# One planned order for all five engines of a four-layer attention kernel, in place of the scheduler's order and a few pins

## The chip, the cores and the metric

One core of a Trainium2 chip. The metric is the device time of one launch in microseconds (us); the kernel before takes 2680.95 us, the median of three runs (2679.22 to 2687.39).

## The reference

An input of 16 samples, each of 256 channels and 32 x 32 positions in float32, goes through four layers, one sample independent of the next. Cut to what matters:

```python
# L0: group norm (8 groups), attention over 1024 positions, projection, residual
xn = group_norm(x, gamma, beta)
q, k, v = split(w_qkv @ xn + b_qkv)
x = w_proj @ (softmax(q.T @ k / 16) applied to v) + b_proj + x
# L1: a gate per position, from the mean and the maximum over the channels
w3 = relu(conv3x3([mean_c(x), max_c(x)], w1, b1))
x = x * sigmoid(conv3x3(mean_c(x) + max_c(x) + w3, w2, b2))
# L2: the same as L0 with its own norm and weights
x = x + wp @ attention(wq @ h, wk @ h, wv @ h) + bp,   h = group_norm(x)
# L3: attention with 32-wide q and k, logits clipped, no norm
energy = clip((Wq @ x + bq).T @ (Wk @ x + bk) * 32**-0.5, -10, 10)
x = gamma[0] * (softmax(energy) applied to Wv @ x + bv) + x
```

## The kernel before

**Weights.** The weights are folded once at the start: the query and key weights of L0 and L2 into one matrix `m`, the value and projection weights into `wvp` (`fold`, `fold3`). A matrix for the 3x3 convolutions, `toep`, is built on POOL from an index table `tidx` (L91 to L101).

**Products.** Nearly all matrix products are made by the Strassen-Winograd scheme: seven products of half-size blocks in place of eight, with sums of blocks before and after. `product` (L577) issues the matmuls; `seven` issues the products of a group in turn, with the names of their PSUM banks: b, a, c, f, with a letter ahead for the stage (sb, sa, sc, sf for the logits, tb, ta, tc, tf for the first projection, vb and so on for the values; b, af, c for the weighted sum). A finished bank is copied to SBUF by ACT (L696 in the logits) or added to a block by DVE (L627 in the logits; L749 in the weighted sum). There are eight banks of PSUM, taken in turn.

**One sample.** `head` loads x (L0's channels, and again as tokens `xr`) and normalises it. `sample` then runs L0's `attend`, the gate of L1, `send`, the group norm of L2, L2's `attend`, `send` again, and L3. In `attend`, `combine` (L924 to L927, DVE) makes the sums `xs` of x's blocks; tb, tc and the others make `t`; `values` makes `vt`; then for each half of the positions `logits` (copies L696, sums L627, exponentials L706 and L708 on ACT) is followed by `weighted` (sums L722, L723, L768, L774 of the exponentials on DVE, copies on ACT, sums L749, and `done`, L754, which scales and adds to the residual). Each half h ends with `then(h, ...)`. In the gate, mean and maximum come from ACT (L1043) and DVE (L1035), and the product with the gate is L1061 on DVE and L1065 on ACT.

**From tokens to channels.** L2 needs channels where L1 left tokens. `turn` transposes with DVE (L525), and `send` writes a half of the sample to DRAM in four pieces and fetches it back in the other layout, all from SP's queue:

```python
            for g in range(NG):
                nc.sync.dma_start(          # L536: mid_x <- t_z or t_l, 128 KB
            ...
            nc.sync.dma_start(              # L540: x <- mid_x, 512 KB
```

**Group norm.** `group_norm` is a chain, most of it on DVE: four `bn_stats` (L114, one for each half and channel block), two aggregates (L117), small steps L119 to L134 with two transposes, then one power on POOL (L138), then three small steps (L141, L143, L144), and the normalisation itself, one half of the channels on DVE (L147) and one on ACT (L150). TensorE's tb product reads what L147 wrote.

**The order of the work.** Even and odd samples are two streams, generators that yield after each product; `in_turn` takes one step of each by turns, the odd stream 30 steps behind (`OFFSET`). Constants `W_...` put further steps between stages. Small tasks without a fixed place, the bias adds (L493, ACT) and the DVE transposes of tokens (L500), are `chores` that are taken one for each step. So the program is written down ("traced") in one order, and from there a scheduler sets each engine's order by its own estimates. It is bound in a few places only: `keep_in_program_order` holds the instructions it is given in their traced order (the building of `toep` on POOL, sample 1's `bn_stats`, the copies of `whole`, parts of `fold3`, a square for the checks on sizes); `behind_folds` puts sample 0's L150 behind the copies of the folded weights on ACT; and `in_traced_order` ties TensorE, DVE and ACT to the traced order in the last sample's `ending`, where the order was written out by hand (L1188 are sums there).

Of the kernel before, what the change touches and what calls it, by code (L numbers as in the profile page):

```python
# [13 lines left out]
ALU = mybir.AluOpType  # L14
AX = mybir.AxisListType

P = 128
C = 256
CC = C // P
# [4 lines left out]
TPH = HALF // P  # L24
GROUP = 32
DQK = 32
G4 = P // DQK
PH = P // 2
# [11 lines left out]
L2_GAMMA, L2_BETA, L2_BQ, L2_BK, L2_BP = range(5, 10)  # L40
NVEC = 10
OFFSET = 30


W_PLANES, W_GATE1, W_GATE2, W_SEND1, W_NORM1, W_NORM2, W_NORM3, W_SEND2, W_EXP, W_AV, W_AV3 = 9, 1, 2, 4, 2, 10, 4, 7, 2, 2, 0
# [6 lines left out]
SIZES = 16384.0  # L52
REACH = 1.0
CHECKS = 3 + 2 * CC


class Const:
# [26 lines left out]
    def build_toep(self, tc, work, tidx):  # L84

        nc = tc.nc
        for k in range(3):
            for tap in range(9):
                w = self.sc[:, S_W1 + 9 * k + tap : S_W1 + 9 * k + tap + 1]
                if tap == 0:  # L90
                    one = self.toep[:, k, :]  # L91
                else:
                    one = work.tile([P, STRIP], FP, tag="tap", name=f"tap_{k}_{tap}")
                tc.keep_in_program_order(
                    nc.gpsimd.tensor_scalar(one, tidx, float(tap), w, ALU.is_equal, ALU.mult)
                )
                if tap:
                    nc.gpsimd.tensor_tensor(self.toep[:, k, :], self.toep[:, k, :], one, ALU.add)
            yield
        for g in range(1, NG):  # L100
            nc.gpsimd.tensor_copy(self.toep[:, 2 + g], self.toep[:, 2])  # L101
        nc.vector.tensor_scalar(self.neg_b2, self.sc[:, S_B2 : S_B2 + 1], -1.0, None, ALU.mult)
        yield


def group_norm(nc, k, small, xt, out, gamma, beta, nm, keep=None, parts=1, behind=None):

    st = small.tile([P, CC, 2, 6], FP, tag="st", name=f"st_{nm}", bufs=2)  # L110
    mv = k.moments
    for c in range(CC):
        for h in range(NH):
            first = nc.vector.bn_stats(st[:, c, h, :], xt[:, c, h * TPH : (h + 1) * TPH])  # L114
            if keep is not None:
                keep(first)
        nc.vector.bn_aggr(mv[:, 2 * c : 2 * c + 2], st[:, c, :, :])  # L117
    row = small.tile([P, GROUP], FP, tag="row", name=f"row_{nm}", bufs=2)
    nc.vector.transpose(row, mv)  # L119
# [20 lines left out]
    a = small.tile([P, CC], FP, tag="a", name=f"a_{nm}")  # L140
# [4 lines left out]
    for i in range(parts):  # L145
        ts = slice(i * NT // parts, (i + 1) * NT // parts)
        nc.vector.tensor_scalar(  # L147
            out[:, 0, ts], xt[:, 0, ts], a[:, 0:1], bb[:, 0:1], ALU.mult, ALU.add
        )
        other = nc.scalar.activation(  # L150
            out[:, 1, ts], xt[:, 1, ts], AF.Identity, bias=bb[:, 1:2], scale=a[:, 1:2]
        )
        if behind is not None:
            behind(other)
    yield


# [50 lines left out]
def fast_path(nc, tc, k, bad, x, w_l0, w_l2, w_l3, qk_bias, v_bias, tap_idx, out):  # L208
# [5 lines left out]

    B = x.shape[0]
    with ExitStack() as ctx:
        wts = ctx.enter_context(tc.tile_pool(name="wts", bufs=1))
        chan = ctx.enter_context(tc.tile_pool(name="chan", bufs=3))
        tokp = ctx.enter_context(tc.tile_pool(name="tokp", bufs=3))
        qkvp = ctx.enter_context(tc.tile_pool(name="qkvp", bufs=2))  # L220
        expp = ctx.enter_context(tc.tile_pool(name="expp", bufs=3))
        combp = ctx.enter_context(tc.tile_pool(name="combp", bufs=2))
        tcp = ctx.enter_context(tc.tile_pool(name="tcp", bufs=2))
        work = ctx.enter_context(tc.tile_pool(name="work", bufs=4))
        small = ctx.enter_context(tc.tile_pool(name="small", bufs=4))
        dram = ctx.enter_context(
            tc.tile_pool(name="dram", bufs=2, space=bass.MemoryType.DRAM)
        )
        ps_m = ctx.enter_context(
            tc.tile_pool(name="ps_m", bufs=8, space=bass.MemoryType.PSUM)  # L230
        )

        def bank(nm):
            return ps_m.tile([P, HALF], FP, tag="m", name=nm)
# [34 lines left out]
        w3 = wts.tile([P, CC, 2 * DQK + C], FP, name="w3")  # L269
# [3 lines left out]
        tidx = wts.tile([P, STRIP], FP, name="tidx")  # L273
# [26 lines left out]
        def whole(w, nm):  # L300

            full = work.tile([P, CC, C], FP, tag="oc", name=f"full_{nm}", bufs=3)
            tc.keep_in_program_order(nc.vector.tensor_copy(full, w))
            nc.vector.tensor_tensor(full[:, 0, P:], w[:, 1, P:], w[:, 0, P:], ALU.subtract)
            return full

        copied = []

        def fold(nm, which, base):


            w = raw[nm]
            wt = expp.tile([P, 3, CC, C], FP, tag="e", name=f"wt_{nm}")

            def transposed(j):
                for o in range(CC):
                    ps = bank(f"wtp_{nm}_{j}_{o}")
                    for c in range(CC):
                        nc.tensor.transpose(
                            ps[:, c * P : (c + 1) * P],  # L320
                            w[:, c, j * C + o * P : j * C + (o + 1) * P],
                            k.ident,
                        )
                    copy = nc.scalar.copy if nm == "l0" else nc.vector.tensor_copy
                    copied.append(copy(wt[:, j, o, :], ps[:, :C]))

            def multiplied(dst, left, right, scale):
                for c in range(CC):
# [82 lines left out]

        def fold3():

            tc.keep_in_program_order(
                nc.vector.tensor_scalar(
                    w3[:, :, :DQK], w3[:, :, :DQK], DQK**-0.5, None, ALU.mult
                )
            )
            for g in (0, G4 - 1):
                s = slice(g * DQK, (g + 1) * DQK)  # L420
                nc.vector.tensor_scalar(qb[s], qb[s], DQK**-0.5, None, ALU.mult)
            for i in range(2):
                for j in range(2):
                    tc.keep_in_program_order(
                        nc.gpsimd.tensor_copy(
                            w3qk[:, :, i, (i ^ j) * DQK : (1 + (i ^ j)) * DQK],
                            w3[:, :, j * DQK : (j + 1) * DQK],
                        )
                    )
            ps = bank("bias3")  # L430
            for c in range(CC):
# [7 lines left out]
            for o in range(CC):  # L439
                for c in range(CC):  # L440
# [4 lines left out]
                        start=(c == 0),  # L445
                        stop=(c == CC - 1),
                    )
            tc.keep_in_program_order(
                nc.vector.tensor_tensor(qb, ps[:, CC : CC + 1], qb, ALU.add)
            )  # L450
            nc.vector.tensor_tensor(bcol3, ps[:, :CC], vcol[:, 2, :], ALU.add)
            nc.vector.scalar_tensor_tensor(bcol3, bcol3, gam, bcol2, ALU.mult, ALU.add)
            in_strips(bcol3, bstrip3, "l3")
# [116 lines left out]
        def product(terms, fresh=True, lone=True):  # L570
# [4 lines left out]
            for i, (out, pairs) in enumerate(terms):  # L575
                for m, (left, right) in enumerate(pairs):
# [10 lines left out]
                    elif m == 0 and not lone:  # L587
# [5 lines left out]
                            ),  # L593
                            reason="the first product clears the bank's flags",
                        )

        def in_traced_order(start):

            engines = mybir.EngineType.PE, mybir.EngineType.DVE, mybir.EngineType.Activation
            before = {}  # L600
            for ins in nc.cur_bb.bb.instructions[start:]:
                if ins.engine not in engines:
                    continue
                if ins.engine in before:
                    tc.add_manual_dep(
                        ins,
                        before[ins.engine],
                        mybir.DependencyInfo(
                            mybir.DependencyClass.NoSync, mybir.DependencyReason.DATA
                        ),  # L610
                        reason="the last sample's order",
                    )
                before[ins.engine] = ins.name

        def seven(go, copy, block, banks, left, right):

# [196 lines left out]
        def alike(w, nm):  # L813


            sq = work.tile([P, HALF], FP, tag="oc", name=f"sq_{nm}", bufs=3)
            tc.keep_in_program_order(
                nc.vector.tensor_tensor(sq.rearrange("p (c o) -> p c o", c=CC), w, w, ALU.mult)
            )
            yield from pause()  # L820
            ps = bank(f"size_{nm}")
            for c in range(CC):
# [169 lines left out]
                then(h, tt.rearrange("p h c n -> p h (c n)"))  # L992
            count(ri, nm)

        def behind_folds(ins):

            tc.add_manual_dep(
                ins.ins,
                copied[-1].ins.name,
                mybir.DependencyInfo(  # L1000
                    mybir.DependencyClass.NoSync, mybir.DependencyReason.DATA
                ),
                reason="the weights' copies come first",
            )

        def head(b):

            fetch(b)
            xt = loaded.pop(b)
            by_chunk = xt.rearrange("p t c n -> p c t n")  # L1010
            xr = tokens[b] = load_tokens(b)
            keep = tc.keep_in_program_order if b == 1 else None
            yield from group_norm(
                nc,
                k,
                small,
                by_chunk,
                by_chunk,
                L0_GAMMA,
                L0_GAMMA + 1,  # L1020
                f"l0_{b}",
                keep,
                1 if b else NH,
                None if b else behind_folds,
            )
            ready[b] = xt, xr

# [68 lines left out]
        def clipped_attend(xt, y, lane, b):  # L1096
# [316 lines left out]
            if b == B - 1:  # L1413
                while running:
                    yield
                start = len(nc.cur_bb.bb.instructions)
                ending()
                in_traced_order(start)
                return

            steps = values(lane, left, right_of(*folded["l3"]), f"l3_{b}")
# [91 lines left out]
        for _ in in_turn([in_turn(streams), rest]):  # L1513
# [7 lines left out]
        nc.vector.tensor_scalar(  # L1521
            bad, some[0:1, :], -1.0, float(P * (3 * B * NT + CHECKS)), ALU.mult, ALU.add
        )


def general_path(nc, tc, k, x, w_l0, w_l2, w_l3, qk_bias, v_bias, out):
# [308 lines left out]
```

## Time and profile before

| what | value |
|---|---|
| median of three runs | 2680.95 us |
| the profiled execution: its own time, span, instructions | 2683.05 us, 2681.3 us, 47925 |
| TensorE (PE) matmuls, busy | 2646.6 us, 99% |
| TensorE weight loads (PEld), busy | 2361.7 us, 88% |
| VectorE (DVE), busy | 2149.9 us, 80%, 4180 instructions |
| ScalarE (ACT), busy | 1332.2 us, 50%, 2825 instructions |
| GpSimd (POOL), busy | 68.5 us, 3%, 172 instructions |
| granted TensorE clock, mean | 0.997 |
| DMA | 123 MB, mean 46 GB/s |
| median from issue to landing: x<-mid_x (512 KB), mid_x<-t (128 KB), x from the input (256 KB), xr (256 KB) | 3.3, 2.3, 4.2, 5.2 us |

The profiled execution is one launch; its span, first to last instruction, is 1.75 us less than its own time. Busy shares are averages over the launch. In a line of the timeline stand the start (us), the duration, the engine, the source line, the operation with its output and inputs, the shape, how many were taken together, and in brackets the idle time before it with what ended it. In the list of waits stand the waiting engine and its work, what released it, and then the idle time in all, how often, and the longest. The same pattern recurs with every pair of samples: eight periods of 328.7 us.

### The profile page before, as it was taken

To read this page: it belongs to the slowest core of one execution; us is meant where nothing else is said; L and a number is where in the kernel's file an instruction comes from. 1 tells how busy PE (TensorE), PEld (TensorE's weight loads), DVE (VectorE), ACT (ScalarE), POOL (GpSimd) and SP (SyncE) were. 2 spreads that over 40 slices of the span, in tenths; PEclk is the share of its full clock that TensorE was granted. 3 is DMA by queue.
4 is the path that set the end of the run, shared out by engine and by line. 5 is a ranking of instruction groups with operands and counts; after the bars stand their busy time and mean duration, and the time that the engine had idled before them with its cause. 6 is when DMAs were issued, how large, how long until landed. Compare 5 with 4: busy or idle time off the path is not lost.

```text
span 2681.3 us, 47925 instructions
## 1 busy us (share of the span) xinstructions
PE 2646.6 (99%) x18998; PEld 2361.7 (88%) x18998; DVE 2149.9 (80%) x4180; ACT 1332.2 (50%) x2825; POOL 68.5 (3%) x172
## 2 busy tenths in 40 slices
PE   8999999999999999999999999999999999999998
PEld 7888898888988889989889898988989889898897
DVE  7888887888778887788867889678887788868776
ACT  4454455544465445554455544554454544545443
POOL 4100000000000000000000000000000000000000
PEclk9999999999999999999999999999999999999999
DMA  4021211212021120211201212112111121101111
GB/s 116 1 64 48 59 29 36 60 40 76 12 55 49 40 72 9 56 48 48 64 17 48 64 34 63 32 32 64 48 48 32 32 64 48 48 17 32 48 40 41
DMA packets 135878, 123.08 MB, mean 46 GB/s; under 512 B 12768, under 2 KB 126688, under 8 KB 135648
## 3 DMA queue, kind: packets, MB, share of 16 engines
q1 hardware_dynamic: 133776, 118.76, 16.1%
q8 instruction: 153, 2.51, 0.4%
q10 hardware_dynamic: 1872, 1.18, 0.1%
q14 instruction: 77, 0.63, 0.1%
HBM read 69.58 MB, written 50.33 MB: 45 GB/s over the span
## 4 chain that ended last, share of the span: by engine, by line
PE 89%; DVE 7%; ACT 1%; issue 1%; DMA 1%; POOL 0%; SPq 0%; DVEq 0%; ACTq 0%
PE b_l L577 16%; PE sb_l L577 12%; PE af_l L577 11%; PE c_l L577 11%; PE sc_l L577 8%; PE vb_l L577 5%; PE sf_l L577 4%; PE sa_l L577 4%; PE vc_l L577 3%; PE tb_l L577 3%; PE s L1135 2%; PE tc_l L577 2%; PE vf_l L577 2%; PE va_l L577 2%; PE qk L1109 1%
## 5 line engine op out<-in xcount | busy, mean ns | idle before, releaser
L577 PE MATMUL sb_l<-t_l,x 128*128 128x256 f32 x1024 | 255.9, 381 | 0.0
L577 PE MATMUL b_l<-vt,e_l 128*128 128x128 f32 x2048 | 250.1, 275 | 0.0
L577 PEld LDWEIGHTS b_l<-vt,e_l 128*128 128x128 f32 x2048 | 242.6, 192 | 4.9 <-DVE acc_l L749 2.3
L696 ACT COPY e_l<-sb_l 128x512 f32<-128x512 f32 x256 | 150.1, 586 | 141.9 <-PE sb_l L577 141.1
L706 ACT ACTIVATE e_l<-e_l 128x512 f32<-128x512 f32 x256 | 159.8, 631 | 121.7 <-DVE e_l L627 119.8
L577 PEld LDWEIGHTS sb_l<-t_l,x 128*128 128x128 f32 x1024 | 185.4, 191 | 32.2 <-issue 10.3
L708 ACT ACTIVATE e_l<-e_l 128x1024 f32<-128x1024 f32 x128 | 135.2, 1056 | 114.3 <-DVE e_l L627 113.6
L627 DVE TENSOR_TENSOR e_l<-sc_l,e_l 128x512 f32<-128x512 f32 x128 | 88.0, 687 | 125.4 <-PE sc_l L577 98.7
L577 PE MATMUL c_l<-tv,cb_l 128*128 128x129 f32 x1504 | 185.8, 276 | 0.0
L577 PEld LDWEIGHTS c_l<-tv,cb_l 128*128 128x128 f32 x1504 | 176.5, 191 | 6.8 <-issue 5.7
L627 DVE TENSOR_TENSOR e_l<-sb_l,e_l 128x512 f32<-128x512 f32 x256 | 165.7, 680 | 4.8 <-ACT e_l L696 0.5
L493 ACT ACTIVATE xr<-xr,bstrip 128x128 f32<-128x128 f32 (+1 forms) x376 | 138.1, 435 | 50.6 <-DVE xr L500 50.6
L773 ACT COPY acc_l<-af_l 128x256 f32<-128x256 f32 x94 | 34.8, 371 | 231.7 <-DVE acc_l L749 231.7
L1151 ACT ACTIVATE e<-s 128x512 f32<-128x512 f32 x256 | 131.5, 598 | 32.4 <-PE s L1135 31.7
L577 PE MATMUL sc_l<-t_l,xs_l 128*128 128x256 f32 x512 | 133.1, 382 | 0.3
L577 PE MATMUL sb_l<-tc_l,xs_l 128*128 128x256 f32 x512 | 132.9, 382 | 0.0
L577 PE MATMUL sf_l<-tc_l,x 128*128 128x256 f32 x512 | 132.5, 382 | 0.0
L577 PE MATMUL sc_l<-tc_l,xs_l 128*128 128x256 f32 x512 | 132.4, 381 | 0.0
L577 PE MATMUL af_l<-tv,e_l 128*128 128x128 f32 x1024 | 129.2, 277 | 2.3 <-ACT e_l L706 2.3
L577 PE MATMUL sa_l<-t_l,x 128*128 128x256 f32 x512 | 131.4, 379 | 0.0
L577 PE MATMUL b_l<-tv,e_l 128*128 128x128 f32 x1024 | 128.0, 275 | 0.0
L577 PEld LDWEIGHTS af_l<-tv,e_l 128*128 128x128 f32 x1024 | 120.5, 192 | 8.0 <-ACT e_l L706 4.9
(304 smaller groups left out, 5919.4 us busy)
## 6 DMA issues: line engine op xcount, KB each, us to landing
x<-mid_x SPq DMA_DIRECT2D x64, 512.0 KB, 3.3
xr<-in_x_dram SPq DMA_DIRECT2D x64, 256.0 KB, 5.2
mid_x<-t_z SPq DMA_DIRECT2D x128, 128.0 KB, 2.3
mid_x<-t_l SPq DMA_DIRECT2D x128, 128.0 KB, 2.3
x<-in_x_dram SPq DMA_DIRECT2D x62, 256.0 KB, 4.2
out_dram<-xr SPq DMA_DIRECT2D x124, 128.0 KB, 2.3
raw_l<-in_w_l_dram SPq DMA_DIRECT2D x1, 1024.0 KB, 7.9
raw_l<-in_w_l_dram SPq DMA_DIRECT2D x2, 256.0 KB, 6.0
```

Of the source, the lines that this page charges most:

```text
L493: nc.scalar.activation(y[:, s, ts], y[:, s, ts], AF.Identity, bias=bias[:, s : s + 1])
L577: mm = nc.tensor.matmul(out, left, right, start=fresh and m == 0 and (lone or i == 0), stop=(m == len(pairs) - 1), skip_group_check=True,)
L627: nc.vector.tensor_tensor(dst, src, dst, ALU.add)
L696: nc.scalar.copy(block(i, j), ps.rearrange("p (m n) -> p m n", m=2))
L706: nc.scalar.activation(part, part, AF.Exp)
L708: nc.scalar.activation(e[:, m : m + 2, :], e[:, m : m + 2, :], AF.Exp)
L773: nc.scalar.copy(acc[:, hi, c1], af[:, 1])
L1109: nc.tensor.matmul(ps[i * PH : (i + 1) * PH, : qt * P].rearrange("p (g n) -> p g n", g=qt), w3qk[:, c, i], xt[:, g0 : g0 + qt, c], start=( ...
L1135: nc.tensor.matmul(ss[g][:, j * 2 * P : (j + 1) * 2 * P].rearrange("p (t g j) -> p t g j", t=TPH, g=2), qk[gs, mh, 1 - blk, j * P : (j + 1 ...
L1151: nc.scalar.activation(by_strip[:, :, :, qa], ss[g].rearrange("p (m t n) -> p m t n", m=2, t=TPH), AF.Exp,)
```

## The change

After the whole program has been traced, a planner works out a time for each instruction, and the resulting order is tied on all five engines. No operation is added or left out.

- `Book` and `Recorded` wrap the tile pools and note for each tile its pool, its tag and the number of buffers.
- `durations` gives each instruction two times in ns: how long it holds its engine (`issue`), and until its result is there (`done`). For a DMA these are fixed values by direction and size.
- `Plan` finds which instructions depend on which, by the regions of the tiles they touch. `run` walks through time: TensorE's products stay in traced order; DVE, ACT, POOL and SP each take the instruction that can start earliest, and among those within 1 ns of each other the one of lowest rank. A tile can be taken only when one of its tag's buffers is free.
- `needed` goes back through the plan and gives each instruction the time by which TensorE needs what follows from it; these times are the ranks of the next round. `pin` makes three rounds (the first has no due times), takes the one that ends first on TensorE, and ties each engine's instructions in its order, one behind the other, without semaphores.
- The uses of `keep_in_program_order`, `behind_folds` and `in_traced_order` are removed.

```diff
+SEEN = 44, 23, 23, 100, 60
+RESTART, ENTRY, MARGIN = 102, 93, 1.04
...
+def durations(engine, ins, outs, reads, mode):
...
+        return max(224, 1.66 * n + 8), max(287, 0.84 * n + 178)
+    if ins.opcode == "DMACopy":
+        if "DRAM" in str(outs[0].tensor.space):
+            return 480, 2500
+        if n == 1024:
+            return 480, 4600
+        return 600, 5600 if n == 512 else 7200
+    if engine == POOL:
+        return 460 + 2 * n, 640 + 2 * n
...
+        for _ in range(n):
+            best = None
+            if at < len(products) and not missing[products[at]]:
+                r = ready(products[at])
+                if r is not None:
+                    best = max(free[PE], r), products[at]
+            for e in (DVE, ACT, POOL, SP):
+                times = [(max(free[e], r), i) for i in waiting[e] for r in [ready(i)] if r is not None]
+                if times:
+                    t = min(times)[0]
+                    i = min((rank[i], i) for u, i in times if u <= t + 1)[1]
+                    if best is None or t < best[0]:
+                        best = t, i
...
+    def needed(self, begin):
...
+            if s.engine == PE:
+                need[i] = begin[i]
+                continue
+            for j in s.ahead:
+                other = self.steps[j].engine
+                last = s.issue if other == s.engine else s.done + SEEN[other]
+                need[i] = min(need[i], need[j] - last)
...
+        best, rank = None, [(0.0, i) for i in range(len(self.steps))]
+        for _ in range(ROUNDS):
+            found = self.run(rank)
+            if best is None or found[0] < best[0]:
+                best = found
+            rank = self.needed(found[2])
+        self.total = best[0]
+        for order in best[1]:
+            for i, j in zip(order, order[1:]):
+                tc.add_manual_dep(
...
+                    reason="the planned order",
...
-            first = nc.vector.bn_stats(st[:, c, h, :], xt[:, c, h * TPH : (h + 1) * TPH])
-            if keep is not None:
-                keep(first)
+            nc.vector.bn_stats(st[:, c, h, :], xt[:, c, h * TPH : (h + 1) * TPH])
...
-                start = len(nc.cur_bb.bb.instructions)
                 ending()
-                in_traced_order(start)
                 return
...
+        Plan(nc, book).pin(tc)
```

## The prediction

> **What bounds it now.** I read the busy table, the waits of TensorE, the timeline around the longest of them, and SyncE's issues there, in that order. (SP is SyncE's queue; a product is one go of a bank: 4 matmul passes of 256 columns, 2 of 512 or 16 of 128.)
>
> ```profile
> PE 2646.6 (99%) x18998; PEld 2361.7 (88%) x18998; DVE 2149.9 (80%) x4180; ACT 1332.2 (50%) x2825; POOL 68.5 (3%) x172
> ...
> PE 89%; DVE 7%; ACT 1%; issue 1%; DMA 1%; POOL 0%; SPq 0%; DVEq 0%; ACTq 0%
> ```
>
> TensorE is busy 99% and is 89% of the chain that ended last: only its idle time can be won, 2681.3 - 2646.6 = 34.7 us and what modelled ends hide. Who makes it wait:
>
> ```profile
> PE tb_l L577 <- issue: 8.5, 8, 1.1
> ...
> PE tb_l L577 <- DVE xs_l L925: 3.0, 8, 0.4
> PE af_l L577 <- ACT e_l L706: 2.3, 8, 0.6
> ```
>
> Eight times each, once per pair of samples: the places recur every 328.7 us. The longest of them, the group norm's last step (L147) that it waits for, and the two at the other sample's norm:
>
> ```profile
> 207.64 1.12 PE L577 MATMUL sb_l<-tc_l,xs_l 128*128 128x256 f32 x4
> 209.82 1.10 PE L577 MATMUL tb_l<-x,m_l 128*128 128x512 f32 x2 [1.06 <-issue]
> ...
> 208.91 0.81 DVE L147 TENSOR_SCALAR x<-x,a_l,bb_l 128x1024 f32<-128x1024 f32 x1
> ...
> 162.89 1.02 PE L577 MATMUL tc_l<-xs_l,mc_l 128*128 128x512 f32 x2
> 164.31 1.10 PE L577 MATMUL tb_l<-xs_l,mc_l 128*128 128x512 f32 x2 [0.40 <-DVE xs_l L925]
> ...
> 166.19 1.13 PE L577 MATMUL tc_l<-xs_l,m_l 128*128 128x512 f32 x2
> 167.43 1.10 PE L577 MATMUL tb_l<-x,m_l 128*128 128x512 f32 x2
> ```
>
> Starts say more than ends. Undisturbed, four 256-column or two 512-column passes take 0.86 us (neighbouring rows). So tb was due at 207.64 + 0.86 = 208.50 and began at 209.82: 1.32 us lost, 0.10 after DVE's L147 had written the normalised x. The others: 164.31 - 163.75 = 0.56 and 167.43 - 167.05 = 0.38, behind L925 and L927, which follow the other sample's norm. **2.26 us a period, 18.1 us in all, wait for the second group norm.** The norm is late because DVE does it last, even where DVE idles and x is there:
>
> ```profile
> 472.88 0.69 DVE L627 TENSOR_TENSOR e_l<-sa_l,e_l 128x512 f32<-128x512 f32 x1 [0.51 <-PE sa_l L577]
> 476.34 0.69 DVE L627 TENSOR_TENSOR e_l<-sc_l,e_l 128x512 f32<-128x512 f32 x1 [2.76 <-PE sc_l L577]
> 476.94 1.28 DVE L114 BATCH_NORM_STATS2 st_l<-x 128x6 f32<-128x512 f32 x2
> ...
> 464.16 3.82 SPq L536 DMA_DIRECT2D mid_x<-t_z  x6
> 468.21 0.34 SPq L540 DMA_DIRECT2D x<-mid_x  x1
> 468.60 0.90 SPq L536 DMA_DIRECT2D mid_x<-t_z  x2
> 473.74 0.34 SPq L540 DMA_DIRECT2D x<-mid_x  x1
> ```
>
> DVE idles 2.76 us. The second half of x could not be fetched before 473.74, because two of its writes to DRAM were issued behind the first half's fetch.
>
> [...] the last writes land 4.6 to 4.8 us after issue, against 2.3 (median) elsewhere. [...]
>
> **The change, part by part** (instruction orders of the two programs side by side).
>
> *No work changes.* Every matmul, DVE, ACT and POOL operation and DMA is there in both; only order and semaphore waits differ.
>
> *TensorE* takes the traced order. 97% of its 9515 products keep their place and the rest move by at most 20. The moves exchange products of the same stage: 0 us. It has 58 more wait instructions; the trace has no price for one. If none were hidden, at some 0.05 us each (estimate: about the smallest DVE steps seen) 2.9 us; in a queue that waits for TensorE anyway, 0. I take 0.
>
> *Even place (470 to 490).* The pinned DVE list puts all four L114, L117 and L119 ahead of the L627 at 476.34, L122 and L124 ahead of the next two, and the rest through L134 ahead of L722; L141 to L147 come after L768. SP now issues all four writes of half two before either fetch. Writes at 467.2 to 468.5 land 2.3 later, at 470.8; the fetch of half one (issued 468.9) takes 3.4 to 4.1, to about 472.5; half two behind it, 512 KB at the 3.1 us between such landings (estimate), to **475.6**. One t_z transpose also moves up by up to 1 us, so 474.6 to 475.6. DVE then: one L114 at 473.5; three from 474.6 or 475.6 (3 x 0.6), 0.35 of small steps; L627 at 476.8 to 477.8 (before 476.34), 0.4 of L122 and L124, then the L627 that feeds the exponential and af, at 477.8 to 478.8 (before 478.14). So af is 0 to 0.6 late; I take **0.3, x 8 = +2.4 us**. Next: L722 ends by 481.9 for c at 482.8; L768 by 484.4 for b at 484.6; then 1.3 us of L141 to L147, L774 by 486.8 for c at 486.3 plus that same 0.3 to 0.6: just covered. The norm is done by 485.7 instead of 489.5.
>
> *Odd place (195 to 210).* 7.1 us of DVE work that stood before L147 now follows it: five L627 (3.1), four L754 (1.7), two L525 (1.2), three L749 and L784 (1.2). Its x half lands by 194.5 (issue 191.2 plus 3.3); three L114, 1.2 of L774, 1.6 of small steps, 0.9 for POOL, 1.3 of L141 to L147 give about 200.5, with tb due at 208.5. The stall at tb goes, and with L924 to L927 4 us earlier at the even place those behind L925 and L927 go: **-18.1 us**. Late instead: the displaced L627, about 3.7 minus 1.8 of filled idle; its exponentials feed products some 8 us on. L754 and L525 send half one of x2, which waits for half two.
>
> *ACT.* Eight L493 (3.2 us) move ahead of three accumulator copies and a bank copy at 433 to 440; ACT idles 5.2 us there: 0. L150 (1.1) moves ahead of L696 in a 4 us hole: 0.
>
> *Start.* vec is fetched before x, so tbp loses its 1.70 us wait (-1.7). But DVE has w3's scale (L415) and qb (L421) ahead of L924, and they wait for w_l3 and the bias loads, behind 1 MB of w_l2[...]: about 17.3 (w_l2 took 5.0 us beyond the load before it, from 11.1, plus 0.9 and 0.3), so L924 at 17.7, not 16.97. POOL builds toep before sample 1's rstd (L138): tidx lands near 21.5, 17 steps of 0.4 or 0.25 to 0.7 us make 7 to 9.5, so 29 to 31; its input comes about then. Taken: **-0.5**, between -3 and +4.
>
> *Tail.* TensorE's list is unchanged, but an L500 (1.16) and an L1188 (0.69) go ahead of xs where DVE waits 1.6 us for x: **+0.2**.
>
> Sum: -18.1 + 2.4 - 0.5 + 0.2 = **-16.0 us** on the profiled execution's 2683.05 (span 2681.3), 2667.0. That execution is 2.1 above the median of 2680.95, so the median comes to **2665**. What a measurement of this kernel can tell is about 0.3%, 8 us.
>
> **Rivals.**
> (a) *The stalls only change place.* DVE is 80% full, so 7.1 us of displaced work could make the exponentials late. For: af already waits for L706. Against: the 8 us of slack. If af and the copies give back 1.3 us more a period (10 us): 2675, no change.
> (b) *Slower: a pinned load that lands too late.* L114 now stands ahead of L627, L722, L768 and L774, and a late half two holds them all. The point: each us beyond about 475 costs 1 us a period, 8 us in all. From 477 the gain is gone; from 478 (+24) it is slower by 8: 2689 and above. For: half two landed at 477.1 before (issue 473.74 plus 3.4), and [...] it gives a fetch 4.6 us alone. Against: the writes no longer queue behind the fetch, and 4.6 is longer than the 3.3 median, so the plan leaves room.
> (c) *More is won:* af's waits (some 0.3 us at 14 places, 4.5), small ones at sc behind L696 (1.6) and the fold's 1.3 go too, with a start 3 better: 2652 to 2655.
>
> **Chances.** Forecast with (c) 0.71, (a) 0.13, (b) 0.16. The forecast's own range is 2652 to 2673; with (a), and (b) down to its point, 2651 to 2690.
>
> **What would show it.** Right: no TensorE wait at tb behind issue or L925, L147 some 7 us earlier at the odd place, both fetches issued after all eight writes, DVE's 2.76 us hole filled. Wrong: a DVE wait at L114 for a DMA above 1.5 us per period, with a new TensorE wait at af or c behind L706, L722 or L774; or a DVE wait for w_l3 past 18 us.

## The result, and the profile after

The changed kernel takes 2657.58 us (median of 6 runs, 2656.41 to 2658.37), the kernel before 2680.25 (6 runs): a ratio of 0.9912, 95% interval 0.9899 to 0.9925. That is 22.7 us less. The two profiled executions are 26.7 us apart (spans 2681.3 and 2654.6), because the one before lay 2.8 us above its median and the one after 1.2 below.

In the changed kernel the line numbers are other ones: `product` is L862 (L577 before), the sums of `seven` L894 (L627), `bn_stats` L408 (L114), the normalisation L439 (L147), the copies and exponentials of the logits L963 and L973 (L696 and L706), the writes and the fetch of `send` L821 and L825. The page after, busy times and the chain that ended last (the chain of work that is followed back from the last instruction):

```profile
PE 2629.1 (99%) x18998; PEld 2366.1 (89%) x18998; DVE 2192.8 (83%) x4180; ACT 1341.7 (51%) x2825; POOL 72.1 (3%) x172
...
PE 97%; DVE 2%; ACT 0%; DMA 0%; issue 0%; DVEq 0%; ACTq 0%
```

The chain is now 97% TensorE, 89% before. The time that DVE, ACT and transfers held it has mostly gone. Who makes TensorE wait now:

```profile
PE reach_l L1132 <- DVE msq_l L1118: 4.7, 1, 4.7
PE fold_l L622 <- DVE wt_l L616: 4.6, 1, 4.6
PE wtp_l L610 <- DMA raw_l<-in_w_l_dram: 4.5, 1, 4.5
PE vb_end L862 <- ACT vt L1436: 1.3, 1, 1.3
PE tb_l L862 <- DVE x L439: 0.7, 1, 0.7
```

Everything that came eight times is gone. What is left occurs once, at the start or at the end. The largest, at reach, is new; the one at fold was 1.3 us before. To see where the time went I took the start of the same product in both traces and added up, stage by stage, how the distance between them changed (after less before):

| stretch of the program | change |
|---|---|
| first 100 us | +8.3 us |
| 100 to 2600 us | -31.9 us |
| the rest | -3.7 us |

The three sum to -27.3 us up to TensorE's last product, and 0.6 us is lost behind it. Within the middle: tb behind the norm (`tb<-x`) -12.9, tb behind the sums (`tb<-xs`) -4.3, af -5.9, sc -3.7, sb -1.5, all others -3.6. Where products have changed places this split is good to about half a us.

**The odd place after** (the timeline of TensorE and of DVE; before, L147 stood at 208.91 and tb waited for it):

```profile
204.87 0.81 DVE L439 TENSOR_SCALAR x<-x,a_l,bb_l 128x1024 f32<-128x1024 f32 x1
...
212.32 1.03 PE L862 MATMUL sa_l<-t_l,x 128*128 128x256 f32 x4
213.19 1.02 PE L862 MATMUL tb_l<-x,m_l 128*128 128x512 f32 x2
```

tb starts 0.87 us after sa, the pitch of four passes, so it waits for nothing. TensorE stood 5.6 us later here than before, because of the start; measured against it, L439 came 208.91 + 5.6 - 204.87 = 9.6 us earlier.

**The even place after**, one period later than the one shown of before (SyncE's issues, then DVE, ACT and TensorE):

```profile
792.03 3.75 SPq L821 DMA_DIRECT2D mid_x<-t_z  x8
796.02 2.49 SPq L825 DMA_DIRECT2D x<-mid_x  x2
...
800.77 0.69 DVE L894 TENSOR_TENSOR e_l<-sa_l,e_l 128x512 f32<-128x512 f32 x1 [0.51 <-PE sa_l L862]
801.38 2.46 DVE L408 BATCH_NORM_STATS2 st_l<-x 128x6 f32<-128x512 f32 x4
...
805.15 1.26 DVE L894 TENSOR_TENSOR e_l<-sb_l,e_l 128x512 f32<-128x512 f32 x2
...
805.85 1.23 ACT L973 ACTIVATE e_l<-e_l 128x512 f32<-128x512 f32 x2 [0.26 <-DVE e_l L894]
806.98 0.35 ACT L1032 COPY acc_l<-b_l 128x256 f32<-128x256 f32 x1
...
806.60 1.95 PE L862 MATMUL af_l<-tv,e_l 128*128 128x128 f32 x16
```

All eight writes go ahead of both fetches; all four L408 lie in the hole of 2.76 us; the exponentials that af reads follow each other, with bank b's copy behind them. Before, two of the four L114 stood directly ahead of those sums, and the copy between the exponentials; the same period before (DVE, then ACT):

```profile
805.70 1.28 DVE L114 BATCH_NORM_STATS2 st_l<-x 128x6 f32<-128x512 f32 x2
806.90 1.27 DVE L627 TENSOR_TENSOR e_l<-sb_l,e_l 128x512 f32<-128x512 f32 x2
...
807.61 0.63 ACT L706 ACTIVATE e_l<-e_l 128x512 f32<-128x512 f32 x1 [1.15 <-DVE e_l L627]
808.14 0.36 ACT L765 COPY acc_l<-b_l 128x256 f32<-128x256 f32 x1
808.39 0.63 ACT L706 ACTIVATE e_l<-e_l 128x512 f32<-128x512 f32 x1
```

**The start after**, on DVE and on TensorE:

```profile
74.95 0.41 DVE L1096 COPY sz_l<-size_l 128x256 f32<-128x256 f32 x1
75.29 0.42 DVE L596 COPY full_m_l<-m_l 128x512 f32<-128x512 f32 x1
...
76.07 0.88 DVE L1118 SCALAR_TENSOR_TENSOR msq_l<-full_m_l,g_l 128x256 f32<-128x256 f32 x2
...
70.99 1.03 PE L862 MATMUL sa_l<-t_l,x 128*128 128x256 f32 x4
76.70 1.71 PE L1132 MATMUL reach_l<-msq_l,ones 128*128 128x256 f32 x4 [4.68 <-DVE msq_l L1118]
```

and by windows, where the granted clock is the third figure from the end of a line (the others are the busy times of the engines, and transfers):

```profile
36.20:40.00 3.80, 3.77 (x10) 3.09 (x11) 3.77 (x7) 0.07 (x1) 3.31 (x7) 0.56 0.00 0
...
76.70:81.00 4.30, 4.30 (x12) 3.16 (x13) 3.37 (x12) 1.78 (x9) 0.19 (x1) 0.60 0.00 0
```

reach belongs to the checks on the sizes of the weights. It waits for msq, msq for full_m, and full_m came right behind the copy L1096, which no product needs. The windows follow the two long waits. In both the clock is down, so at reach four passes take 1.71 us in place of 1.03: the 4.7 us wait put TensorE 6.7 us back (from 1.6 to 8.3 us behind the kernel before).

### The profile page after: what moved, and what is told of

It is laid out like the page before. It is cut to its first block, busy times and chain, and to the rows that moved or that the text cites. A ratio compares the mean times of both kernels' runs of the same rounds, so it can differ in the third digit from the quotient of the medians.

```text
span 2654.6 us, 47938 instructions
## 1 busy us (share of the span) xinstructions
PE 2629.1 (99%) x18998; PEld 2366.1 (89%) x18998; DVE 2192.8 (83%) x4180; ACT 1341.7 (51%) x2825; POOL 72.1 (3%) x172
## 4 chain that ended last, share of the span: by engine, by line
PE 97%; DVE 2%; ACT 0%; DMA 0%; issue 0%; DVEq 0%; ACTq 0%
PE b_l L862 19%; PE c_l L862 13%; PE af_l L862 13%; PE sb_l L862 13%; PE sc_l L862 8%; PE vb_l L862 5%; PE sf_l L862 4%; PE sa_l L862 4%; PE vc_l L862 3%; PE tb_l L862 3%; PE s L1386 3%; PE tc_l L862 2%; PE vf_l L862 2%; PE va_l L862 2%; PE qk L1360 1%; PE tf_l L862 1%
## 5 line engine op out<-in xcount | busy, mean ns | idle before, releaser
L862 PE MATMUL sb_l<-t_l,x 128*128 128x256 f32 x1024 | 255.3, 381 | 0.0
L862 PE MATMUL b_l<-vt,e_l 128*128 128x128 f32 x2048 | 250.1, 275 | 0.0
L862 PEld LDWEIGHTS b_l<-vt,e_l 128*128 128x128 f32 x2048 | 242.6, 192 | 4.9 <-issue 2.3
L973 ACT ACTIVATE e_l<-e_l 128x512 f32<-128x512 f32 x256 | 159.0, 630 | 130.0 <-DVE e_l L894 128.1
L862 PEld LDWEIGHTS sb_l<-t_l,x 128*128 128x128 f32 x1024 | 185.2, 190 | 32.0 <-issue 10.3
L963 ACT COPY e_l<-sb_l 128x512 f32<-128x512 f32 x256 | 149.6, 585 | 119.2 <-PE sb_l L862 117.8
L862 PE MATMUL c_l<-tv,cb_l 128*128 128x129 f32 x1504 | 185.8, 276 | 0.0
L894 DVE TENSOR_TENSOR e_l<-sc_l,e_l 128x512 f32<-128x512 f32 x128 | 87.8, 686 | 116.2 <-PE sc_l L862 87.7
L862 PEld LDWEIGHTS c_l<-tv,cb_l 128*128 128x128 f32 x1504 | 176.5, 191 | 6.8 <-PE qk L1360 3.1
L894 DVE TENSOR_TENSOR e_l<-sb_l,e_l 128x512 f32<-128x512 f32 x256 | 164.2, 681 | 4.2 <-PE sb_l L862 1.3
L778 ACT ACTIVATE xr<-xr,bstrip 128x128 f32<-128x128 f32 (+1 forms) x376 | 140.4, 437 | 25.5 <-DVE xr L785 13.9
L862 PE MATMUL sc_l<-tc_l,xs_l 128*128 128x256 f32 x512 | 133.0, 382 | 0.0
L862 PE MATMUL sf_l<-tc_l,x 128*128 128x256 f32 x512 | 132.5, 382 | 0.0
L862 PE MATMUL sc_l<-t_l,xs_l 128*128 128x256 f32 x512 | 132.2, 381 | 0.0
L862 PE MATMUL sb_l<-tc_l,xs_l 128*128 128x256 f32 x512 | 131.4, 379 | 0.0
L862 PE MATMUL sa_l<-t_l,x 128*128 128x256 f32 x512 | 131.4, 379 | 0.0
L862 PE MATMUL af_l<-tv,e_l 128*128 128x128 f32 x1024 | 125.7, 275 | 0.0
L862 PE MATMUL c_l<-vt,e_l 128*128 128x129 f32 x1024 | 125.7, 275 | 0.0
L862 PE MATMUL af_l<-vt,e_l 128*128 128x128 f32 x1024 | 125.5, 276 | 0.0
L862 PE MATMUL b_l<-tv,e_l 128*128 128x128 f32 x1024 | 125.4, 275 | 0.0
```

The lines of the kernel that those rows point to most:

```text
L778: nc.scalar.activation(y[:, s, ts], y[:, s, ts], AF.Identity, bias=bias[:, s : s + 1])
L862: mm = nc.tensor.matmul(out, left, right, start=fresh and m == 0 and (lone or i == 0), stop=(m == len(pairs) - 1), skip_group_check=True,)
L894: nc.vector.tensor_tensor(dst, src, dst, ALU.add)
L963: nc.scalar.copy(block(i, j), ps.rearrange("p (m n) -> p m n", m=2))
L973: nc.scalar.activation(part, part, AF.Exp)
```

## The experiments

Times are medians; the ratio is to the kernel before on the same chip, with its 95% interval.

| run | what is tied | us | ratio |
|---|---|---|---|
| the changed kernel | all five engines, the whole program | 2657.6 | 0.9912 (0.9899 to 0.9925) |
| mid_all | all five, in the middle only | 2648.9 | 0.9887 (0.9871 to 0.9904) |
| mid_all_tail | the same, and the end | 2647.4 | 0.9878 (0.9862 to 0.9895) |
| mid_no_sp | TensorE, DVE, ACT, POOL, middle | 2662.7 | 0.9935 (0.9919 to 0.9952) |
| mid_dve_act_sp | DVE, ACT, SP, middle | 2663.4 | 0.9934 (0.9917 to 0.9950) |
| mid_dve_sp | DVE, SP, middle | 2692.6 | 1.0056 (1.0040 to 1.0073) |
| mid_dve | DVE, middle | 2700.9 | 1.0078 (1.0061 to 1.0095) |
| mid_sp | SP, middle | 2682.2 | 1.0008 (0.9999 to 1.0016) |
| due_oc | all; one tag's buffers have due times | 2650.3 | 0.9893 (0.9876 to 0.9909) |
| due_buffers | all; every tag's buffers have due times | 2703.1 | 1.0087 (1.0071 to 1.0104) |
| one_round | all; no due times | 2705.5 | 1.0098 (1.0081 to 1.0115) |
| land_seen | all; transfers near their medians, token loads below theirs | 2680.5 | 0.9999 (0.9990 to 1.0008) |
| land_short | all; transfers under 1 us | 3089.5 | 1.1528 (1.1508 to 1.1548) |

### Where in the program, and which engines

These kernels are the kernel before, its own pins kept, with the planner added and `pin` cut down to some engines and to the middle:

```diff
-        for order in best[1]:
+        begin = best[2]
+        for e, order in enumerate(best[1]):
+            if e not in PINNED:
+                continue
+            order = [
+                i
+                for i in order
+                if begin[i] >= FROM and (TAIL or self.steps[i].at < self.book.ending)
+            ]
             for i, j in zip(order, order[1:]):
```

`FROM` is 100 us of the plan's time, `book.ending` the place where the last sample's `ending` begins. In their profiles `product` is L888, the sums L938, `bn_stats` L422, the exponentials L1017, the copies of the logits L1007 and of bank b L1076, the fetch L851.

**mid_all: all five engines.**

> The kernel before, its start (the first 100 us of the plan) and its last sample left as they were, with the planned order tied on all five engines only in between. Theory: the stretch from 100 to 2600 us gained 31.9 us by itself (TensorE's starts of the same products, after against before), while the start lost 8.3 and the end won 3.7; so 2680 - 32 = 2648 (2645 to 2652), faster than the full plan by some 9 less 4 us, 4 or more. Rival: the work that the plan pushed out of the start pays for the later gain, so that they can't be had apart: 2656 to 2660.

Measured 2648.9, as the theory had it; the products of the middle gained 31.5 us. So the middle's gain does not need the start, and the start's loss is one of its own. (The start differs by a few us from one profiled run of these kernels to another, so small parts of it are rough.)

**mid_dve, mid_sp and mid_dve_sp.**

> As mid_all, but only DVE's order is tied; SP still issues half one's fetch ahead of half two's last two writes. Theory (the prediction's slower case): half two lands some 2 to 3 us later than under the plan, and the four L114 that the plan puts early hold DVE that long, 8 times: 18 us won at tb, 16 to 24 lost behind L114, so 2676 to 2690. Rival: DVE's order alone makes the gain, and its 2.8 us hole swallows the later landing: 2650 to 2656.

> As mid_all, but only SP's order is tied: all eight writes before either fetch, DVE's and ACT's order from the scheduler. Theory: x is there 2.7 us earlier, but DVE still takes the norm last, so tb waits as before: 2676 to 2681. Rival: the late landing is what makes the norm late: the 18 us at tb go, 2660 to 2664.

> As mid_all, with DVE's and SP's orders tied, ACT's, POOL's and TensorE's free. Theory: tb's 18 us and the part of af's and sc's waits that comes from DVE (about 6) go; what is left to ACT's order is some 8: 2654 to 2659. Rival: ACT and TensorE follow by themselves, all 32 us are DVE's and SP's: 2646 to 2650.

mid_sp gains nothing (2682.2, 1.2 us above the theory's range): an earlier x is worth nothing where DVE takes the norm last, and tb still waits 9.6 us in all. mid_dve is slower, and by more than the theory said; L422 waits 18.4 us for transfers in it. mid_dve_sp refutes theory and rival alike: 2692.6, where I had 2646 to 2659. tb's waits did go (-20.6 us over the middle), but af lost 14.9 and other products 15 more. Its even place, ACT, DVE and TensorE:

```profile
478.17 0.37 ACT L1076 COPY acc_l<-b_l 128x256 f32<-128x256 f32 x1 [2.92 <-PE b_l L888]
478.44 1.67 ACT L1017 ACTIVATE e_l<-e_l 128x512 f32<-128x512 f32 x3
...
476.51 1.25 DVE L938 TENSOR_TENSOR e_l<-sb_l,e_l 128x512 f32<-128x512 f32 x2
...
479.64 1.60 PE L888 MATMUL af_l<-tv,e_l 128*128 128x128 f32 x12 [1.06 <-ACT e_l L1017]
```

DVE has the plan's order, and its sums are ready by 477.8. But ACT, ordered by the scheduler, has the copy of bank b at the head of its queue. The copy waits for TensorE's b until 478.17, ACT idles 2.92 us, and the three exponentials behind it, ready to run, make af wait. An order is good only together with the others' orders. So ACT was tied as well:

> As mid_dve_sp (2692.6), with ACT's order tied too; TensorE and POOL stay free. Theory: the 44 us between mid_dve_sp and mid_all (2648.9) are ACT's: there the scheduler put the copy of bank b, which waits for TensorE, ahead of three exponentials that were ready, and af waited behind them; with ACT tied that goes: 2647 to 2653. Rival: TensorE's own order (9% of its products stand elsewhere when it is free) makes a good part of the 44: 2660 to 2685.

Measured 2663.4. Tying ACT too is worth 29.2 us by the medians (2692.6 - 2663.4), 33 by the ratios, and af's waits are gone, as the theory said; but the rival holds for what is left down to mid_all, 14.5 us by the medians and 13 by the ratios, which belongs to the order of TensorE or POOL. An engine that is left free does not keep its old order: by the starts in the traces 97% of TensorE's passes stand where they stood before in mid_all, 93% in mid_dve_sp, 91% in mid_dve_act_sp. So each of these steps is the tie together with what the free engines then did. The line of TensorE's waits that came with it:

```profile
PE sb_l L888 <- ACT e_l L1007: 3.5, 8, 0.4
```

The rest is spread over many products that stand a place apart and wait a little. Which of the two engines' ties does it was not tried; POOL has only the norms' powers and the counts in the middle, and no wait of TensorE that was listed names it there.

### SP's part: the slower case by itself

> As mid_all (2648.9), with SP's order alone left to the scheduler, so that half one's fetch again stands ahead of half two's last two writes. Theory (the prediction's slower case, by itself): half two lands some 2.7 us later and the pinned L114 hold the sums L627 behind them; mid_dve against mid_dve_sp says 8 to 10 us over the launch: 2656 to 2661, and TensorE waits at af or sc. Rival: with ACT's order right, DVE's hole takes up the delay: 2648 to 2651.

Measured 2662.7, 13.8 us above mid_all, so the theory holds, and the price is higher than it said. SyncE, DVE and TensorE at the even place:

```profile
458.91 2.73 SPq L847 DMA_DIRECT2D mid_x<-t_z  x6
462.68 0.34 SPq L851 DMA_DIRECT2D x<-mid_x  x1
463.07 0.90 SPq L847 DMA_DIRECT2D mid_x<-t_z  x2
467.21 0.34 SPq L851 DMA_DIRECT2D x<-mid_x  x1
...
470.59 1.29 DVE L422 BATCH_NORM_STATS2 st_l<-x 128x6 f32<-128x512 f32 x2 [1.05 <-DMA x<-mid_x]
...
474.55 1.60 PE L888 MATMUL af_l<-tv,e_l 128*128 128x128 f32 x12 [0.46 <-ACT e_l L1017]
```

The second fetch is issued only at 467.21, DVE stands at L422 for half two, and af waits behind that. Over the launch L422 waits 21.2 us (16 times, up to 2.9), in mid_all 1.4.

### The plan's values for transfers

```diff
-            return 480, 2500
+            return 480, 2300
         if n == 1024:
-            return 480, 4600
-        return 600, 5600 if n == 512 else 7200
+            return 480, 3500
+        return 480, 4000 if n == 512 else 4000
```

> The changed kernel with the plan's transfers at about the medians of the trace: to DRAM 2300 ns (2500), fetch of 512 KB 3500 (4600), the others 4000 (5600, 7200). Theory: half two's real landing is 3.65 us after its issue and its last write's 2.76, so L114 comes before x in part of the 16 norms, by up to 0.6 us each, and the longer first loads are misjudged by 2 us and more at the start: 2660 to 2675. Rival: nearer to the real landings the plan is truer and what it loses by waits it wins by an earlier norm: 2650 to 2658.

Measured 2680.5: the whole gain is gone, 5 us beyond the theory's range. DVE's wait for transfers at `bn_stats` and TensorE's waits in land_seen:

```profile
DVE st_l L408 <- DMA x<-mid_x: 13.0, 15, 2.1
...
PE vc_l L862 <- ACT vt L1212: 12.2, 7, 2.3
PE af_l L862 <- ACT e_l L973: 6.8, 8, 1.8
```

and DVE's in the changed kernel:

```profile
DVE st_l L408 <- DMA x<-mid_x: 0.4, 1, 0.4
```

Two transfers are at fault. For `bn_stats`, and af behind it, the reason is in the landings of the 16 fetches of half two that feed L2's norm. In the changed kernel they take 3.65 to 4.57 us from issue, median 4.19; in land_seen 4.00 to 5.5. The plan's 4.6 us lies above all of the changed kernel's; 3.5 us, the median over all 64 fetches, lies below the fastest. But this is the smaller part: by the starts, the middle lost 30.1 us against the changed kernel, 8.9 of it at af and 14.1 at vc. The waits at vc come from the token loads `xr`. ACT and TensorE at one of the seven places:

```profile
1006.06 0.91 ACT L778 ACTIVATE xr<-xr,bstrip 128x256 f32<-128x256 f32 x2 [4.66 <-DMA xr<-in_x_dram]
1006.87 0.57 ACT L1212 COPY vt<-vc_l 128x512 f32<-128x512 f32 x1
...
1007.49 1.16 PE L862 MATMUL vc_l<-wvp_l,xs_l 128*128 128x128 f32 x8 [2.25 <-ACT vt L1212]
```

The plan put a bias add (L778) there with the load taken at 4.0 us, in place of 7.2 in the changed kernel. In the middle of land_seen 39 of the 52 token loads take longer, up to 6.1 us. ACT stands at the add for 3.4 to 4.7 us at each of these places, and the copy of vt behind it keeps vc waiting. The run changed all the values at once, so what each is worth alone was not tried. In land_short (issue 60, landing 600 or 800 ns) both faults are larger:

> The changed kernel with short transfers in its plan: issue 60 ns and landing 600 or 800 ns in place of 480 to 600 and 2500 to 7200. Theory: the plan then puts L114 (and what reads the tokens) ahead of the sums long before x can be there, DVE waits for the transfer with the sums behind it, at least 1 us at each of 16 norms: 2668 to 2690. Rival: DVE's spare time and the pinned order of the rest hide it: 2655 to 2660, no difference from the changed kernel's 2657.6.

Measured 3089.5, some 400 us beyond the theory. DVE waits 142.5 us for transfers at L406 (`bn_stats` there) and 90.6 at the sums xs, ACT 122.2 at the bias adds of the token loads (L776 there), and TensorE behind them. ACT and TensorE at one such place, where it is the token load:

```profile
481.38 1.31 ACT L776 ACTIVATE xr<-xr,bstrip 128x256 f32<-128x256 f32 x3 [9.71 <-DMA xr<-in_x_dram]
...
484.25 2.07 PE L860 MATMUL vb_l<-vc_l,xs_l 128*128 128x128 f32 x8 [8.56 <-ACT vt L1210]
486.11 3.62 PE L860 MATMUL b_l<-vt,e_l 128*128 128x128 f32 x16
```

and the window behind the wait, with the clock third from the end:

```profile
484.00:490.00 6.00, 5.75 (x27) 5.76 (x28) 3.54 (x6) 3.50 (x9) 0.00 (x0) 0.50 0.02 4
```

After a wait of 8.56 us the clock is at half: 16 passes take 3.62 us in place of 1.95. The mean clock of the launch is 0.942, against 0.997.

### The due times

one_round is `ROUNDS = 1`.

> The changed kernel with one round in place of three: each engine takes what can start earliest, ties in traced order, without due times. Theory: where DVE has a queue, a norm's step or a transpose that nobody waits for goes ahead of a sum that TensorE waits for; the waits at af, sc and tb come back in part: 2666 to 2680. Rival: it is the tie of the orders to each other that counts, not the due times: 2655 to 2661.

Measured 2705.5. Ties alone, in an order made without due times, are worse than the scheduler's order. TensorE's waits in it:

```profile
PE b_l L862 <- DVE e_l L1035: 18.5, 8, 2.9
PE af_l L862 <- ACT e_l L973: 8.9, 8, 1.5
```

At 194 to 199 us of its timeline DVE runs the whole chain of a norm, L408 to L426, ahead of the sum L1035 that b waits for.

due_buffers adds, for each tag, a due time from a tile's first user back to the users of the tiles ahead of it:

```diff
+                for j in {first[at - 1], *(self.users[old] if at >= book.bufs(name) else ())}:
+                    if j < first[at]:
+                        self.later.setdefault(j, []).append(first[at])
...
-            for j in s.ahead:
+            for j in s.ahead + self.later.get(i, []):
```

> The changed kernel with one more rule in `needed`: the due time of a tile's first user also goes back to those who must have taken or left the tag's earlier tiles. Theory: TensorE's wait of 4.7 us at reach (76.7 us) is the copy L1096, which no product needs and which therefore goes last in DVE's queue, while the buffer order of its tag holds full_m, msq and mdg behind it; with a due time for it the wait goes: 2651 to 2654. Rival: DVE is full from 61 to 77 us, so another product waits in its place: 2656 to 2660.

Measured 2703.1, far above what theory and rival said. The start did what the theory says: reach no longer waits, and TensorE is 5.0 us ahead of the changed kernel at 90 us. But the middle lost 48 us, in two places that come seven and eight times:

```profile
PE s L1399 <- DVE vt L907: 18.5, 7, 2.7
PE c_l L875 <- ACT acc_l L1058: 11.4, 8, 1.9
```

s does not read vt; what L907 reads is a bank of PSUM, so s seems to wait for that bank. After the one of these waits at s that ends at 353.3 us, 2.63 us long, the clock is down (0.51 from 355.1 to 358.6 us: two passes of sa take 1.06 us there, where four take 1.03). The mean clock of the launch is 0.993, against 0.997 in the changed kernel, and the products behind s lost 11.5 us more. Why the plan takes this order to be good was not settled. due_oc applies the rule to the one tag `oc` alone:

> As due_buffers, with the added due times for the one tag `oc` alone (full_m, msq, mdg, the copies of the checks). Theory: the wait of 4.7 us at reach goes as it did in due_buffers (TensorE was 5.0 us ahead of the changed kernel at 90 us there), and without the other tags' due times the middle stays as in the changed kernel: 2650 to 2654. Rival: any other plan of the start shifts the later order too and runs into new waits for banks, as due_buffers did from 150 us on: over 2665.

Measured 2650.3; in the middle the starts agree with the changed kernel's to 0.2 us, and the start is 8.7 us better. DVE and TensorE at the place:

```profile
56.60 0.41 DVE L1111 COPY sz_l<-size_l 128x256 f32<-128x256 f32 x1
60.65 0.42 DVE L611 COPY full_m_l<-m_l 128x512 f32<-128x512 f32 x1
...
69.03 1.03 PE L877 MATMUL sa_l<-t_l,x 128*128 128x256 f32 x4
69.89 1.03 PE L1147 MATMUL reach_l<-msq_l,ones 128*128 128x256 f32 x4
```

The copy that nobody had a due time for (L1111 here) moved from 74.95 to 56.60, and reach follows sa at once. So the reach wait was a fault of `needed`: due times go through data, not through the buffers that a tile must wait for. The wait of fold, 4.4 us here too, stays. In the changed kernel DVE is busy for 4.9 of the 5.2 us ahead of it, among other things with the norm's chain through L439, and its copies for fold take no longer than before (two in 0.75 us, 0.73 before). That speaks for its order, but no run changed it.

### The end

> As mid_all (2648.9), with the last sample tied by the plan too, in place of the order written by hand. Theory: the full plan won 3.7 to 3.9 us there (s<-t_qk 2.9, vb_end 1.1, qk 0.85, less 1 elsewhere): 2644 to 2646. Rival: the end's gain needs the order that the plan gave ahead of it and what follows is late: 2648 to 2651.

Measured 2647.4, 1.5 us below mid_all. In the profiled executions s at the end gained 3.4 us, as expected, but the medians' intervals overlap, so the size is open. Of all versions tried mid_all_tail has the lowest median, 10 us below the changed kernel; due_oc is 7 below, with an interval that overlaps the changed kernel's.

## Why the prediction was right, and where not

The prediction was 2665 (2651 to 2690), faster; measured 2657.6. Its main step held; the other terms did not. That the middle's 8.8 us of unforeseen gain at sc, sb and the smaller products and the start's 8.8 us of unforeseen loss cancel is luck: without the start's loss the result would have been near 2649 us, as mid_all's 2648.9 shows, and below the range.

- **tb, -18.1 us: right.** Measured -17.2 (12.9 + 4.3). The stated signs came: no wait of the middle at tb, L147 earlier at the odd place by 9.6 us (some 7 foretold), both fetches behind all writes, the hole filled. mid_dve and mid_dve_sp show that DVE's order takes these waits away, with SP's tied or not, and also that this alone makes the kernel slower.
- **af, +2.4 us: wrong in sign; measured -5.9.** The step took 474.6 to 475.6 for half two's landing. It landed at 801.82, which on the kernel before's clock and one period earlier is 474.0 (801.82 + 0.9 - 328.7; TensorE was 0.9 us ahead there). The larger fault: the step took the sums' times before as the measure, though its own fence shows two L114 at 476.94, ahead of the next of them. Those went into the hole, so the sums came earlier than before, and the copy of bank b moved behind the exponentials.
- **ACT and TensorE, 0 us: wrong.** sc, sb and the smaller products gained 8.8 us more. The step asked whether ACT has time for the moved work; it has. What counts is what stands at the head of its queue: with DVE and SP tied, tying ACT is worth some 30 us, and TensorE with POOL another 13 to 15. "97% keep their place" was no measure of the price.
- **Start, -0.5 us: wrong; measured +8.3**, outside its -3 to +4. TensorE was 2.4 us ahead at 20 us, and neither w_l3 nor `toep` made TensorE wait. The two waits that decided, at fold (net 4.0) and at reach (6.7 with the slow clock), the prediction did not have: its comparison of orders looked at the group norms and loads and not at the checks.
- **Tail, +0.2 us: wrong; measured -3.7.** The sums ahead of xs cost little (TensorE waits 0.6 us for xs there), and s no longer waits 2.1 us, with the clock at 0.54 behind it.
- **Rival (b), slower: real, but not in this kernel.** mid_no_sp is that mechanism alone and costs 13.8 us; it still beats the kernel before. land_seen shows it again: with the fetch planned at its median the middle lost 8.9 us at af, besides what the token loads cost. The prediction's reason, that 4.6 is longer than the median of 3.3, pointed the right way, but the fetches that matter take 4.19 in the median, so the room is 0.4 us and not 1.3. A few landings beyond the planned value cost little: mid_all_tail, the run with the lowest median, has two of 4.68 and 4.93 us, and DVE waits 1.3 us in all at `bn_stats` for these fetches.
- **Rival (a), the waits only change place:** it came true where only DVE and SP are tied. **Rival (c), more is won:** its term at af came nearly as listed (4.5 foretold, 5.9 measured) and the one at sc was twice as large (1.6 and 3.7); its better start and fold's 1.3 did not come.

## What to carry to other kernels

The engines' queues are one schedule: a planned order tied on one engine made this kernel slower (DVE, +21 us), the same order tied on all made it 31 us faster. In such a plan a transfer's value must not lie below what that transfer usually takes at the place where its data are awaited: 4.6 us for the fetch and 7.2 for the token loads did not, 3.5 and 4.0 did. An instruction planned too early holds everything behind it, as the bias adds of land_seen held ACT, for 3.4 to 4.7 us at each of seven places. Whether still longer values do better was not tried. Work without a due time sinks to the end of a full queue, so what holds a buffer that others need must inherit their due time. That helped for the one tag where the wait was found; the same rule for every tag made the kernel slower.

## What the runs showed of the hardware

**A wait of TensorE cost more than itself.** The 4.7 us at reach put TensorE 6.7 us back. After the waits of 4.6 and 4.7 us in the changed kernel and of 8.56 us in land_short the granted clock over the next 3.8 to 6 us was 0.56, 0.60 and 0.50. Shorter waits were followed by a low clock too: one of 2.63 us in due_buffers (0.51 from 355.1 to 358.6 us), the one of 2.1 us at s near the end of the kernel before (0.54 from 2636.5 to 2644.0 us) and the one of 0.93 us at strips at its start (0.50 from 46.2 to 49.6 us). Two others were not: the kernel before's 1.28 us at fold (1.00 from 35.3 to 39.0 us) and one of 2.25 us in land_seen (1.00 from 1007.5 to 1012.0 us). So in these runs the length of a wait alone does not say whether the clock goes down behind it; what decides it was not shown. I had priced the start's waits by their length alone.

**A fetch of 512 KB took longer while another was under way.** Half two's took 4.19 us (median of 16) in the changed kernel, with half one's issued 2.1 us ahead, and 3.32 in the kernel before, where half one's had landed. In mid_sp, where SP's order alone is tied and the fetches are again 2.1 us apart, it was 4.15.
